# Where the survey of the weights' groups and the spread of zero points stand in the first projection of a fused attention and GPTQ block

## Chip, cores and metric

One core of a Trainium2 chip. The metric is the device time of one execution in microseconds; lower is better. Three runs of the kernel before gave 2293.84 to 2294.37 us, median 2293.89.

## Reference

One block over x of shape (2, 1024, 1024). The normalized input goes through causal attention (32 query heads and 8 key and value heads of 32) and, beside it, through a gated MLP whose weights are packed in 4 bits with scales and zero points by group. The result is x plus the product of the two.

```python
xn = _layernorm(x, axis=-1)
s = _L0_attn_ref(xn, wq, wk, wv, wo)          # q, k with rope; causal softmax; out @ wo
g = _silu(_L0_ffn_ref(xn, ...))
x = x + s * g

# in _L0_ffn_ref
w_gu = _dequant(qweight_gu, qzeros_gu, scales_gu, g_idx_gu)
gate, up = (inter[..., :INTER], inter[..., INTER:])   # inter = xn @ w_gu, INTER = 2752
h = jax.nn.silu(gate) * up
w_d = _dequant(qweight_down, qzeros_down, scales_down, g_idx_down)
# out = h @ w_d
# _dequant: W[i,j] = sc[g[i],j] * (wq[i,j] - (zq[g[i],j] + 1)), 4-bit wq and zq unpacked by shifts
```

The group index of a row is data. The kernel looks at it: if each row is in the group of its place and the scales lie in a safe range, a fast path multiplies by integers and applies ratios of scales to the sums; otherwise a general path runs.

## The kernel before

Each of the two batches goes through normalization, projection, attention and output projection; the MLP of both follows at the end. The change touches the first batch's projection.

`project` does 20 turns in that batch: four for the keys (two blocks of 512 tokens by two chunks of columns), then eight chunks of queries by two blocks. One call of `turned` makes a turn or two of them: eight fp32 products of 128x512 into a PSUM tile `ps_qk` (three buffers), on VectorE a multiplication (rot1, L388) and a shuffle (rot2, L390), on GpSimd two operations (L391, L392), on ScalarE a cast `rot_hi` (L394), on VectorE the rest `rot_lo` (L396), and on SyncE two stores. After each query chunk `xnT` is split in the same way into `x_hi` (ScalarE, L439) and `x_lo` (VectorE, L440), stored by SyncE. From the third chunk on, between the products, `head.rows()` makes the first head's scores `s` (L554, masks L548), whose maxima VectorE reads (L564); at the end of each half a transposition `m_ps` (L599) follows. At last `values(t)` makes eight value tiles `ps_v` (L407, two PSUM buffers), each copied by ScalarE into `v` (L410). Attention (`attend`) begins with products `st` (L661, L676), whose exponentials ScalarE takes (L686); the maxima of the next head come from `kst` and `qst`, loaded by SyncE (L508, L513).

At the end of each turn one step of the generator `look` is taken, behind the turn's last instructions: `next(side, None)` under `behind(turn)`. `look` has 12 steps: four of `survey` for the gate and up weights (zero points unpacked, negated and stored as two bytes in `z_gu`; scales tested; group indices tested), four for the down weights (`z_d`), one that spreads `z_gu` over the 128 rows of `zb_gu` by eight DRAM to DRAM copies, one that spreads `z_d` over `zb_d` by 21, one for `scales_turned` (scales transposed on TensorE, reciprocals and ratios on VectorE), and one for the flag that chooses the path. `unpack` reads `zb_gu` and `zb_d` from the first output projection on.

Within a stage a scheduling layer places the instructions of all engines: products of `values` are drawn forward or left at the end according to what it thinks ready. Each engine then works strictly in its order. A DMA is an instruction in the queue of the engine that issues it: the spread copies are ScalarE's, nearly everything else here is SyncE's. Tiles loaded in `look` have a buffer of their own; `psp` has one PSUM buffer for the transposed scales and the flag's sum.

Of the kernel before, what the change touches and what calls it, by code (L numbers as in the profile page):

```python
# [10 lines left out]
F32 = mybir.dt.float32  # L11
# [5 lines left out]
I32 = mybir.dt.int32  # L17
AF = mybir.ActivationFunctionType
ALU = mybir.AluOpType
AX = mybir.AxisListType  # L20
# [3 lines left out]
P = 128  # L24
# [12 lines left out]
def block_kernel(  # L37
# [18 lines left out]
    nc = tc.nc  # L56
    B, T, D = x.shape
# [7 lines left out]
    G_D = sc_d.shape[0]  # L65
# [13 lines left out]
    ones_f = const.tile([P, HD], F32, name="ones_f")  # L79
# [9 lines left out]
    flag = const.tile([1, 1], I32, name="flag")  # L89
# [19 lines left out]
    z_gu = dram.tile([G_GU, 2 * INTER, 2], U16, name="z_gu")  # L109
    z_d = dram.tile([G_D, D, 2], U16, name="z_d")  # L110
# [14 lines left out]
    def survey(pool, bad, sc, qz, gi, z_dram, col, tag):  # L125

        g, n = sc.shape
        rows = gi.shape[0]
        w = g * n // 8 // P
        words = pool.tile([P, w], U32, name=f"words_{tag}")  # L130
        nc.sync.dma_start(words, qz.rearrange("g n -> (g n)").rearrange("(p w) -> p w", p=P))
        z = pool.tile([P, w, 8], U32, name=f"z_{tag}")
        for j in range(8):
            nc.vector.tensor_scalar(z[:, :, j], words, 4 * j, 15, ALU.logical_shift_right, ALU.bitwise_and)
        yield
        zf = pool.tile([P, 8 * w], F32, name=f"zf_{tag}")
        nc.vector.tensor_scalar(zf, z.rearrange("p w j -> p (w j)"), -257.0, 15.0 * 257.0, ALU.mult, ALU.add)
        zc = pool.tile([P, 8 * w, 2], U16, name=f"zc_{tag}")
        for i in range(2):
            nc.vector.tensor_copy(zc[:, :, i], zf)  # L140
        nc.sync.dma_start(z_dram.rearrange("g n i -> (g n i)").rearrange("(p w) -> p w", p=P), zc.rearrange("p w i -> p (w i)"))
        yield

        scale = pool.tile([P, 8 * w], F32, name=f"scale_{tag}")
        nc.sync.dma_start(scale, sc.rearrange("g n -> (g n)").rearrange("(p w) -> p w", p=P))
        nc.vector.tensor_tensor(scale, scale, scale, ALU.mult)
        top = pool.tile([P, 8 * w], F32, name=f"top_{tag}")
        nc.vector.tensor_scalar(top, scale, SC_MAX * SC_MAX, None, ALU.is_le)
        nc.vector.tensor_scalar(scale, scale, SC_MIN * SC_MIN, None, ALU.is_ge)
        nc.vector.tensor_tensor(scale, scale, top, ALU.mult)  # L150
        nc.vector.tensor_scalar(scale, scale, -1.0, 1.0, ALU.mult, ALU.add)
        nc.vector.tensor_reduce(bad[:, col : col + 1], scale, AX.X, ALU.add)
        yield

        k = 64
        m = rows // k
        idx = pool.tile([k, m], I32, name=f"idx_{tag}")
        nc.sync.dma_start(idx, gi.rearrange("(p m) -> p m", p=k))
        at = pool.tile([k, m], F32, name=f"at_{tag}")
        nc.vector.tensor_copy(at, idx)  # L160
        wrap = pool.tile([k, m], F32, name=f"wrap_{tag}")
        nc.vector.tensor_scalar(wrap, at, 0.0, float(g), ALU.is_lt, ALU.mult)
        nc.vector.tensor_add(at, at, wrap)
        nc.vector.tensor_scalar(at, at, 0.0, float(g - 1), ALU.max, ALU.min)
        row = pool.tile([k, m], I32, name=f"row_{tag}")
        nc.gpsimd.iota(row, pattern=[[1, m]], base=0, channel_multiplier=m)
        nc.vector.tensor_scalar(row, row, 7, None, ALU.logical_shift_right)
        want = pool.tile([k, m], F32, name=f"want_{tag}")
        nc.vector.tensor_copy(want, row)
        nc.vector.tensor_scalar(want, want, float(g - 1), None, ALU.min)  # L170
        nc.vector.tensor_tensor(at, at, want, ALU.not_equal)
        nc.vector.tensor_reduce(bad[:k, col + 1 : col + 2], at, AX.X, ALU.add)
        yield

    def scales_turned(pool, psp):
        by_u = pool.tile([2 * G_GU, NF * P], F32, name="by_u")
        for u in range(2):
            nc.sync.dma_start(
                by_u[u * G_GU : (u + 1) * G_GU, : NF * P - P], sc_gu[:, u * INTER : u * INTER + NF * P - P]
            )  # L180
        tail = pool.tile([G_GU, P], F32, name="tail")
        for u in range(2):
            nc.sync.dma_start(
                tail[:, u * FTAIL : (u + 1) * FTAIL], sc_gu[:, (u + 1) * INTER - FTAIL : (u + 1) * INTER]
            )
        ps = psp.tile([P, NF, 2, G_GU], F32, name="ps_sc", tag="ps")
        for f in range(NF - 1):
            nc.tensor.transpose(
                ps[:, f].rearrange("p u g -> p (u g)"),
                by_u[:, f * P : (f + 1) * P],  # L190
                ident[: 2 * G_GU, : 2 * G_GU],
            )
        for u in range(2):
            nc.tensor.transpose(ps[:, NF - 1, u, :], tail, ident[:G_GU, :G_GU])
        inv = pool.tile([P, NF, 2, G_GU], F32, name="inv")
        nc.vector.reciprocal(inv, ps)
        nc.vector.tensor_tensor(r_gu, ps[:, :, :, : G_GU - 1], inv[:, :, :, 1:], ALU.mult)
        nc.vector.tensor_copy(l_gu, ps[:, :, :, G_GU - 1 :])
        by_g = pool.tile([G_D, D], F32, name="by_g")
        nc.sync.dma_start(by_g, sc_d)  # L200
        ps = psp.tile([P, NC, G_D], F32, name="ps_sd", tag="ps")
        for c in range(NC):
            nc.tensor.transpose(ps[:, c, :], by_g[:, c * P : (c + 1) * P], ident[:G_D, :G_D])
        inv = pool.tile([P, NC, G_D], F32, name="inv_d")
        nc.vector.reciprocal(inv, ps)
        nc.vector.tensor_tensor(r_d, ps[:, :, : G_D - 1], inv[:, :, 1:], ALU.mult)
        nc.vector.tensor_copy(l_d, ps[:, :, G_D - 1 :])

    def look(pool, psp):

        bad = pool.tile([P, 4], F32, name="bad")
        nc.vector.memset(bad, 0.0)
        yield from survey(pool, bad, sc_gu, qz_gu, gi_gu, z_gu, 0, "gu")
        yield from survey(pool, bad, sc_d, qz_d, gi_d, z_d, 2, "d")
        for g in range(G_GU):
            r0 = g * (P // G_GU)
            r1 = r0 + P // G_GU
            nc.scalar.dma_start(zb_gu[r0:r1], z_gu[g : g + 1].to_broadcast([r1 - r0, 2 * INTER, 2]))
        yield
        for g in range(G_D):  # L220
            r0 = g * 16
            r1 = r0 + 16 if g < G_D - 1 else RD
            nc.scalar.dma_start(zb_d[r0:r1], z_d[g : g + 1].to_broadcast([r1 - r0, D, 2]))
        yield
        scales_turned(pool, psp)
        yield
        one = pool.tile([P, 1], F32, name="one")
        nc.vector.tensor_reduce(one, bad, AX.X, ALU.add)
        ps = psp.tile([1, 1], F32, name="ps_bad", tag="ps")
        nc.tensor.matmul(ps, one, ones_f[:, :1], start=True, stop=True)  # L230
        nc.vector.tensor_scalar(flag, ps, 1.0, None, ALU.min)
        yield

    def unpack(pool, gu, down):
# [1212 lines left out]
    for b in range(B):  # L1447
# [5 lines left out]
        with tc.tile_pool(name="at_first", bufs=1, reuse_waits="tile") as fp, tc.tile_pool(  # L1453
            name="qkv_T", bufs=1, reuse_waits="tile"
# [4 lines left out]
            with tc.tile_pool(name="ps_s", bufs=1, space=PSUM, reuse_waits="tile") as ps_s:  # L1459
                head = Maxima(qs_dram[b], ks_dram[b], fp, ps_s, room)  # L1460
                if b == 0:
                    with tc.tile_pool(name="prep", bufs=1) as pool, tc.tile_pool(
                        name="prep_ps", bufs=1, space=PSUM
# [83 lines left out]
```

## Time and profile before

| what | us |
|---|---|
| median of three runs | 2293.89 |
| the profiled execution's own time | 2293.33 |
| its span in the profile | 2291.6 |
| TensorE busy | 2239.3 |
| VectorE, ScalarE, GpSimd busy | 1420.2, 1132.3, 792.4 |
| first product of the first projection starts | 26.9 |
| first product of the first attention starts | 220.4 |

A row of the timeline gives start, duration, engine, line, operation, tiles and count, and in brackets how long the engine was idle before it and what ended that. Rows marked ACTq and SPq are DMA instructions in the queues of ScalarE and SyncE; the duration of a merged row includes the waits between its instructions. An fp32 product shows as two passes in TensorE's rows. The table of stretches gives, for each engine, busy time and the number of instructions, then TensorE's granted clock (1.00 is full), the share of the DMA engines' time that is busy, and GB/s.

### The profile page before, as it was taken

Reading aid. Unit: us, or ns where it says so; the run is one execution under the profiler, and the core shown is the slowest. Engines: PE = TensorE matmul, PEld = TensorE weight load, DVE = VectorE, ACT = ScalarE, POOL = GpSimd, SP = SyncE. Lnnn points to the kernel's source line nnn. Section 1 sums busy time; section 2 is a strip of 40 time slices with the busy share of each in tenths; the row PEclk is TensorE's granted clock in tenths of the full one; section 3 lists DMA queues with packets and bytes.
Section 4 is the critical chain, followed back from the end, with each engine's and each line's share of the span. In section 5 each row is a group of like instructions: output and inputs, shape, how many; then the busy total and the mean of one; then the engine's idle time right before and its main releaser. Section 6 shows DMA issues by size and latency. Waiting matters only on the chain.

```text
span 2291.6 us, 30825 instructions
## 1 busy us (share of the span) xinstructions
PE 2239.3 (98%) x11313; PEld 1537.5 (67%) x11313; DVE 1420.2 (62%) x2268; ACT 1132.3 (49%) x1819; POOL 792.4 (35%) x569
## 2 busy tenths in 40 slices
PE   7989999999999999999999999999999999999998
PEld 4455555555874465555558888888877888888875
DVE  5544677773324736777722367667877777777775
ACT  2102544553223325445533455555887555556875
POOL 1303677774035427776741100000234100001362
PEclk9999999999999999999999999999999999999999
DMA  5727323122468971231319623231846655323475
GB/s 180 220 91 244 80 47 93 38 75 76 129 210 280 301 215 47 52 88 38 80 54 344 181 56 83 55 83 55 303 138 219 176 137 139 96 71 105 137 231 154
DMA packets 262183, 309.50 MB, mean 135 GB/s; under 512 B 19147, under 2 KB 197707, under 8 KB 261880
## 3 DMA queue, kind: packets, MB, share of 16 engines
q1 hardware_dynamic: 245172, 260.62, 38.4%
q0 software_dynamic: 10752, 38.02, 5.2%
q10 hardware_dynamic: 6100, 8.82, 1.2%
q8 instruction: 91, 1.49, 0.3%
q14 instruction: 68, 0.56, 0.1%
HBM read 214.58 MB, written 97.03 MB: 136 GB/s over the span
## 4 chain that ended last, share of the span: by engine, by line
PE 82%; issue 7%; POOL 6%; DVE 2%; ACT 2%; DMA 1%; SPq 0%; ACTq 0%; POOLq 0%; DVEq 0%
PE acc L1198 27%; PE acc L1079 12%; PE ps_wo L880 10%; PE st L661 7%; PE s L554 7%; PE o L708 5%; PE ps_qk L384 5%; PE l L726 3%; PE st L676 2%; PE ps_v L407 1%; POOL rot L391 1%; PE s L548 1%; POOL rot L392 1%; POOL p L821 1%; ACT p L686 1%
## 5 line engine op out<-in xcount | busy, mean ns | idle before, releaser
L1198 PE MATMUL acc<-x,w 128*128 128x512 f32 x2752 | 640.1, 393 | 1.2 <-ACT gate L1169 0.9
L1198 PEld LDWEIGHTS acc<-x,w 128*128 128x128 f32 x2752 | 512.3, 188 | 120.5 <-DVE h L1171 7.2
L564 DVE TENSOR_REDUCE mx<-s 128x1 f32<-128x512 f32 (+3 forms) x672 | 384.8, 608 | 190.3 <-PE s L554 91.7
L968 DVE TENSOR_SCALAR acc<-acc,r_gu 128x1024 f32<-128x1024 f32 x301 | 389.1, 1293 | 166.5 <-PE acc L1198 164.9
L686 ACT ACTIVATE p<-st 128x512 f32<-128x512 f32 (+3 forms) x768 | 314.7, 497 | 316.8 <-PE st L676 314.6
L966 ACT ACTIVATE acc<-acc,r_gu 128x1024 f32<-128x1024 f32 x301 | 327.4, 1088 | 231.5 <-PE acc L1198 226.7
L1182 POOL TENSOR_TENSOR h_lo<-h,h_hi 128x512 fp32r<-128x512 f32 x78 | 100.3, 1287 | 805.2 <-DVE h L1160 300.6
L821 POOL TENSOR_TENSOR p<-p 128x2048 f32<-128x2048 f32 (+3 forms) x122 | 360.0, 2955 | 9.0 <-PE o L708 4.6
L968 DVE TENSOR_SCALAR acc<-acc,r_d 128x512 f32<-128x512 f32 x320 | 241.7, 759 | 62.0 <-PE acc L1079 59.3
L966 ACT ACTIVATE acc<-acc,r_d 128x512 f32<-128x512 f32 x320 | 210.8, 663 | 61.8 <-PE acc L1079 55.0
L384 PE MATMUL ps_qk<-xnT,w_qk 128*128 128x512 f32 x512 | 236.0, 602 | 2.5 <-DVE rot L390 2.5
L880 PE MATMUL ps_wo<-oT,w_o 128*128 128x256 f32 x1024 | 232.1, 382 | 0.0
L1079 PE MATMUL acc<-h_lo,w 128*128 128x512 f32 (+1 forms) x576 | 228.9, 397 | 3.0 <-POOL h_lo L1182 2.6
L1079 PE MATMUL acc<-h_hi,w 128*128 128x512 f32 (+1 forms) x576 | 229.5, 398 | 0.7 <-ACT h_hi L1181 0.7
L880 PEld LDWEIGHTS ps_wo<-oT,w_o 128*128 128x128 f32 x1024 | 191.1, 190 | 40.9 <-issue 16.7
L708 PE MATMUL o<-p,v 128*32 128x512 f32 (+3 forms) x1536 | 162.9, 496 | 0.9 <-POOL p L689 0.9
L384 PEld LDWEIGHTS ps_qk<-xnT,w_qk 128*128 128x128 f32 x512 | 94.6, 192 | 99.8 <-issue 93.4
L689 POOL TENSOR_SCALAR_AFFINE_SELECT p<-p 128x512 f32<-128x512 f32 x128 | 80.5, 636 | 163.5 <-ACT p L686 123.0
L391 POOL TENSOR_TENSOR rot<-rot,cs 128x512 f32<-128x512 f32 x40 | 51.3, 1283 | 239.6 <-DVE rot L390 230.2
L554 PE MATMUL s<-kst,room 128*128 128x512 f32 (+3 forms) x384 | 130.4, 379 | 0.0
L1079 PEld LDWEIGHTS acc<-h_lo,w 128*128 128x128 f32 (+1 forms) x576 | 108.4, 188 | 31.0 <-POOL h_lo L1182 5.4
L1079 PEld LDWEIGHTS acc<-h_hi,w 128*128 128x128 f32 (+1 forms) x576 | 108.3, 188 | 30.6 <-issue 2.9
(163 smaller groups left out, 2405.7 us busy)
## 6 DMA issues: line engine op xcount, KB each, us to landing
w<-ng SPq DMA_DIRECT2D x86, 512.0 KB, 5.2
w<-nd SPq DMA_DIRECT2D x63, 512.0 KB, 4.0
ng<-nf POOLq DMA_DIRECT2D x42, 512.0 KB, 6.9
room<-qs SPq DMA_DIRECT2D x160, 128.0 KB, 4.0
x<-xs SPq DMA_DIRECT2D x32, 512.0 KB, 10.2
qst<-qs SPq DMA_DIRECT2D x96, 128.0 KB, 3.8
xt<-in_L_attn_x SPq DMA_DIRECT2D x16, 512.0 KB, 6.2
w_qk<-in_L_attn_wq SPq DMA_DIRECT2D x16, 512.0 KB, 5.0
```

Of the source, the lines that this page charges most:

```text
L384: nc.tensor.matmul(ps, w[:, s, :], xnT[:, s, tok], start=(s == 0), stop=(s == NS - 1))
L554: nc.tensor.matmul(s[:, c * w : (c + 1) * w], q[j][:, qt * P : (qt + 1) * P], k[:, k0:k1], start=n == 1, stop=c == n - 1 and (n > 1 or not ...
L564: nc.vector.tensor_reduce(mx[:, at, js[0] : js[0] + n, k0 // TB], s[:, : w * n].rearrange("p (j t) -> p j t", j=n), AX.X, ALU.max)
L661: nc.tensor.matmul(s[:, q0:], kst[g][:, kt * P : (kt + 1) * P], stack[g][j][:, qlo + q0 : qlo + TB], start=True, stop=False,)
L686: nc.scalar.activation(p[:, j, q0:], st[j][:, q0:], AF.Exp, scale=1.0 / math.sqrt(HD))
L708: nc.tensor.matmul(o[HD * j : HD * (j + 1), q0:], v[:, kt, HD * g : HD * (g + 1)], p[:, j, q0:], start=(kt == 0), stop=last,)
L821: what(*args)
L880: self.last = nc.tensor.matmul(ps[:, c * self.BLK : (c + 1) * self.BLK], self.ws[c0 + c][:, g, :], self.oT[:, g, t0 : t0 + self.BLK], star ...
L966: nc.scalar.mul(a, a, r)
L968: nc.vector.tensor_scalar(a, a, r, None, ALU.mult)
L1079: nc.tensor.matmul(acc[c], w[:k, c * P : (c + 1) * P], ht[:k, :], start=(f == 0 and t == 0), stop=(t == 1), skip_group_check=(f > 0),)
L1198: nc.tensor.matmul(a[:, n, :], w[i][:, g * P : (g + 1) * P], xs[t][:, g, n * TB : (n + 1) * TB], start=(g == 0 and t == 0), stop=(t == 1), ...
```

## The change

`look` is arranged anew, in 20 steps. First come the loads: `survey` and `scales_turned` issue their loads and yield, one after the other, in turns 1 to 3. Then the surveys' arithmetic, turns 4 to 11. Four steps are empty. `scales_turned` becomes a generator of two steps, turns 16 and 17; the flag follows at 18; the spread of `z_gu` comes at turn 19 and that of `z_d` at turn 20, the last.

```diff
@@ survey
+        k = 64
+        m = rows // k
         words = pool.tile([P, w], U32, name=f"words_{tag}")
         nc.sync.dma_start(words, qz.rearrange("g n -> (g n)").rearrange("(p w) -> p w", p=P))
+        scale = pool.tile([P, 8 * w], F32, name=f"scale_{tag}")
+        nc.sync.dma_start(scale, sc.rearrange("g n -> (g n)").rearrange("(p w) -> p w", p=P))
+        idx = pool.tile([k, m], I32, name=f"idx_{tag}")
+        nc.sync.dma_start(idx, gi.rearrange("(p m) -> p m", p=k))
+        yield
...
-        scale = pool.tile([P, 8 * w], F32, name=f"scale_{tag}")
-        nc.sync.dma_start(scale, sc.rearrange("g n -> (g n)").rearrange("(p w) -> p w", p=P))
...
-        k = 64
-        m = rows // k
-        idx = pool.tile([k, m], I32, name=f"idx_{tag}")
-        nc.sync.dma_start(idx, gi.rearrange("(p m) -> p m", p=k))
@@ scales_turned
+        by_g = pool.tile([G_D, D], F32, name="by_g")
+        nc.sync.dma_start(by_g, sc_d)
+        yield
...
-        by_g = pool.tile([G_D, D], F32, name="by_g")
-        nc.sync.dma_start(by_g, sc_d)
+        yield
@@ look
-        yield from survey(pool, bad, sc_gu, qz_gu, gi_gu, z_gu, 0, "gu")
-        yield from survey(pool, bad, sc_d, qz_d, gi_d, z_d, 2, "d")
+        parts = [
+            survey(pool, bad, sc_gu, qz_gu, gi_gu, z_gu, 0, "gu"),
+            survey(pool, bad, sc_d, qz_d, gi_d, z_d, 2, "d"),
+            scales_turned(pool, psp),
+        ]
+        for part in parts:
+            next(part)
+            yield
+        for part in parts[:2]:
+            yield from part
+
+        for _ in range(4):
+            yield
+        yield from parts[2]
+        yield
+        one = pool.tile([P, 1], F32, name="one")
+        nc.vector.tensor_reduce(one, bad, AX.X, ALU.add)
+        ps = psp.tile([1, 1], F32, name="ps_bad", tag="ps")
+        nc.tensor.matmul(ps, one, ones_f[:, :1], start=True, stop=True)
+        nc.vector.tensor_scalar(flag, ps, 1.0, None, ALU.min)
+        yield
         for g in range(G_GU):
...
             nc.scalar.dma_start(zb_gu[r0:r1], z_gu[g : g + 1].to_broadcast([r1 - r0, 2 * INTER, 2]))
         yield
         for g in range(G_D):
...
             nc.scalar.dma_start(zb_d[r0:r1], z_d[g : g + 1].to_broadcast([r1 - r0, D, 2]))
-        yield
-        scales_turned(pool, psp)
-        yield
-        one = pool.tile([P, 1], F32, name="one")
-        nc.vector.tensor_reduce(one, bad, AX.X, ALU.add)
-        ps = psp.tile([1, 1], F32, name="ps_bad", tag="ps")
-        nc.tensor.matmul(ps, one, ones_f[:, :1], start=True, stop=True)
-        nc.vector.tensor_scalar(flag, ps, 1.0, None, ALU.min)
         yield
```

## The prediction

> **What bounds the kernel now.** I read the page first (shares of busy time and the chain that ended last), then a table of stretches over the first projection, then TensorE's timeline there, then ScalarE's and SyncE's queues.
>
> From the page, engine shares and the chain:
>
> ```profile
> PE 2239.3 (98%) x11313; PEld 1537.5 (67%) x11313; DVE 1420.2 (62%) x2268; ACT 1132.3 (49%) x1819; POOL 792.4 (35%) x569
> PE 82%; issue 7%; POOL 6%; DVE 2%; ACT 2%; DMA 1%; SPq 0%; ACTq 0%; POOLq 0%; DVEq 0%
> ```
>
> TensorE is the bound: 2239.3 of 2291.6 us. A change can give only what TensorE sits idle or runs at a low clock, and costs what it adds to that. Stretches of the first projection and of the start of attention behind it (busy time by engine, then the granted clock):
>
> ```profile
> 26.00:82.00 56.00, 56.00 (x132) 25.29 (x131) 21.60 (x69) 6.56 (x12) 17.78 (x15) 0.97 0.42 130
> 82.00:151.00 69.00, 68.94 (x241) 38.46 (x240) 37.36 (x84) 2.99 (x5) 13.11 (x11) 1.00 0.47 147
> 151.00:173.00 22.00, 15.83 (x44) 8.24 (x42) 10.84 (x25) 3.95 (x8) 2.52 (x2) 0.77 0.41 135
> 173.00:220.00 47.00, 46.78 (x157) 28.58 (x156) 22.42 (x42) 10.66 (x21) 18.35 (x14) 1.00 0.69 245
> 220.00:226.00 6.00, 3.57 (x21) 2.55 (x20) 0.36 (x1) 3.72 (x6) 0.64 (x1) 1.00 1.05 238
> ```
>
> TensorE is full except at 151-173 (6.2 us idle, clock 0.77) and at 220-226 (2.4 us). Its timeline there:
>
> ```profile
> 154.12 0.38 PE L599 MATMUL m_ps<-ident_b,mt 128*128 128x128 bf16 x4 [1.39 <-DVE mt L588]
> 156.99 9.70 PE L384 MATMUL ps_qk<-xnT,w_qk 128*128 128x512 f32 x16 [2.49 <-DVE rot L390]
> 168.98 3.68 PE L407 MATMUL ps_v<-w_kv,xnT 128*128 128x256 f32 x8 [2.29 <-ACT v L410]
> 177.93 27.63 PE L384 MATMUL ps_qk<-xnT,w_qk 128*128 128x512 f32 x64
> 225.30 0.47 PE L554 MATMUL s<-kst,qst 128*128 128x128 f32 x2 [1.94 <-DMA qst<-qs]
> ```
>
> Undisturbed, 64 passes take 27.63 us, 0.432 each, so a turn's 16 take 6.9; after the gaps 16 took 9.70. The gaps' cause is on ScalarE: waits of 19.8 and 50.7 us, both on the DMA issues of the zero points' spread.
>
> ```profile
> 94.74 20.33 ACTq L218 DMA_DIRECT2D zb_gu<-z_gu  x8
> 115.17 0.62 ACT L394 CAST rot_hi<-rot 128x512 fp32r<-128x512 f32 x1 [19.82 <-DMA zb_gu<-z_gu]
> 121.37 45.07 ACTq L223 DMA_DIRECT2D zb_d<-z_d  x21
> 166.48 1.14 ACT L439 CAST x_hi<-xnT 128x512 fp32r<-128x512 f32 x2 [50.70 <-DMA zb_d<-z_d]
> ```
>
> A single issue of these rows takes 0.48 to 0.62 us; the rest of 65 us is waiting. For what, the built program says: SyncE and ScalarE share eight DMA semaphores in turn, and each DMA instruction waits until the former DMA on its semaphore has landed, whoever issued it. The queues show it:
>
> ```profile
> 133.29 0.37 SPq L350 DMA_DIRECT2D w_qk<-in_L_attn_wq  x1
> 137.98 0.47 ACTq L223 DMA_DIRECT2D zb_d<-z_d  x1
> 155.59 0.34 SPq L398 DMA_DIRECT2D qs<-rot_lo  x1
> 157.62 0.48 ACTq L223 DMA_DIRECT2D zb_d<-z_d  x1
> ```
>
> The second zb_d copy starts 4.7 us after the weight load that held its semaphore; the ninth, 2.0 us after the store of rot_lo that held its own. Landing times (last column, median us):
>
> ```profile
> room<-qs SPq DMA_DIRECT2D x160, 128.0 KB, 4.0
> qst<-qs SPq DMA_DIRECT2D x96, 128.0 KB, 3.8
> kst<-ks SPq DMA_DIRECT2D x48, 128.0 KB, 2.8
> zb_gu<-z_gu ACTq DMA_DIRECT2D x8, 344.0 KB, 6.0
> ```
>
> **The change part by part.** *Loads first.* Eleven small SyncE loads (0.3 to 0.6 us an issue, but for words_gu, which waits) are issued at turns 1 to 3. Six of them (words, scale, idx) move past each other and past stores of ks; SyncE is mostly idle until 60 us and TensorE runs without a gap to 151. The third w_qk load, issued at 22 us before, now stands behind turn 3's store (about 54 us); it is first used in turn 9, at 26.9 + 8 x 6.87 = 82 us, and lands in 5. Nothing, with 23 us of cover.
>
> *Surveys three turns later, turned scales at turns 16 and 17, flag at 18.* The same VectorE instructions in other turns; GpSimd's two iotas (0.14 us) move with them. VectorE has 5.6 us of work in a turn with rows (rotation 1.4, rot_lo 0.7, x_lo 0.7, four maxima of 0.69) against TensorE's 7.8, but the reciprocals (2.35 and 1.20) now fall among these turns, and the flag's matmul stands in TensorE's order behind a sum that is itself behind a rot_lo. Below: 0. Above: some five gaps like the 1.39 us one for m_ps, 8 us. I take 3.
>
> *The 29 zero-point copies at turns 19 and 20.* Moving them frees 151-173: 1.39 + 2.49 + 2.29 = 6.2 us idle; 9.70 - 6.9 = 2.8 of cold passes; 3.68 - 8 x 0.22 = 1.9 of cold value passes (0.22 is 7.93 us for 36 later). The 2.4 us wait for qst goes too, those loads being issued during the new stall. Gain 13.3.
>
> At their new place ScalarE's order is: rot_hi of turn 19, 8 zb_gu, rot_hi of turn 20, 21 zb_d, two x_hi, then all eight copies of v. Only two value tiles fit in PSUM, so TensorE's third value product waits for the first copy of v. Let T be the end of turn 19 on TensorE. TensorE still has turn 20 (6.9), four m_ps passes (0.4), two value tiles (16 x 0.22 = 3.5 each) and the first st products (1.28 + 0.33): it stops at T + 15.9. In the turns shown, rot_hi starts 4.2 us after its products end (shuffle, two GpSimd steps of 1.26). From there, by the semaphores that the built program names:
> - copy 1 issues at 0 and lands at 6.0; SyncE's fourth qst load waits for it, and four issues later (0.42 each) one leaves at 7.7 that lands at 11.5;
> - copy 4 waits for that, and lands at 17.5; a kst load waits for it, and the third after it leaves at 18.8 and lands at 21.6;
> - copy 7 waits for that, and lands at 27.6; a room load waits for it, and lands at 31.6;
> - the third zb_d waits for that; 19 issues of 0.62 end at 43.4. Copies 8 and 9 of zb_d wait for turn 20's stores, which are due before: turn 20's rot_hi runs at about 26.
> Two x_hi (1.1) and a copy of v (0.4) make 44.9. TensorE goes on at T + 4.2 + 44.9 = T + 49.1: **a stall of 33.2 us**. Nothing hides it: VectorE has no rows left, and the first exponentials stand behind v. Three landings of zb_gu lie on this chain; one of 4 or 8 us, as loads beside it land, makes 27 or 39.
>
> After it: 2.8 us of cold clock as after the old gap, and ScalarE's table load (1.28) and first exponentials, which before ran beside the kst products, hold TensorE about 1.3.
>
> From the first products of attention on, TensorE's instructions stand in the same order to the end, and its idle time at 226-300 is 0.85 us: no slack takes up the delay. Loads done early could win 2 us there at most.
>
> Sum: 33.2 + 2.8 + 1.3 + 3.0 - 13.3 = **+27.0 us**. On the profiled execution: span 2291.6 + 27.0 = 2318.6, plus the 1.7 outside it (2293.33 - 2291.6) is 2320.3; the median of the runs, 2293.89, is 0.6 above that execution: 2321.
>
> **Two rules of the Trainium skill against these rows.** Row: ScalarE held for 20.33 and 45.07 us by 29 copies. "DMA: Bandwidth & Descriptors", section "Issuing engines are not separate DMA queues", says that issuing from several engines saves only the sequencer's issue time, usually small. By that the copies hold ScalarE 29 x 0.62 = 18 us, with the cast, x_hi and v 20.1; the stall is 8.4 and the sum +2.2. The same page says that a semaphore wait happens on the issuing sequencer; the rows show that here, so I take the chain. Row: 16 passes at 9.70 instead of 6.9. "TensorE: Matmul & The Clock Gate", Part 1, has half rate for about 3.4 us after idling: an estimate of 1.7 us lost. The row decides, 2.8; by the rule the sum were 25.9.
>
> **The rivals.** *A: the semaphores do not bite* (SyncE's loads land sooner than zb_gu asks for theirs), and only the issues hold ScalarE for 18 us: +2.2, 2296, and -2 (2292) without the VectorE gaps and the exponentials' wait: not slower. It decides where the copies hold ScalarE less than about 20 us. For: the copies are small. Against: both holds of before. 5%. *B: the old holds come back whole*, 20.3 + 45.1 with the cast between: ScalarE frees v 1.5 us after T + 4.2 + 66.0, the stall is 55.8 and the sum +50, 2344. Against: the 45 us held two waits, for a weight buffer (121.4 to 138.0) and for a rot_lo behind late maxima (to 157.6), and neither stands there now. 8%. *C: the moved copies and the loads share the 16 DMA engines*, 0.69 busy on average before and 1.05 at 220-226; landings of 8 us make +33, 2327. This is inside my range.
>
> **How the numbers follow.** A difference below 0.2% (4.6 us) is not told from none. Stall with its chain, C included: 87%, from +15 (landings 4, no VectorE gaps, early loads help) to +38; its likeliest value is 2321. A's 5% divides into 2% within 0.2%, 3% faster. B 8%. Slower: 95%. Eight in ten: 2305 to 2336.
>
> **What would show it.** In the profile after: no gap at 151-173 and clock 1.0 there; one TensorE gap of 27 to 39 us before a ps_v of L421, ended by the copy of v on ScalarE; zb_gu's eight issues spread over about 25 us and zb_d's 21 over some 14, at about 0.62 each; qst loads of SyncE broken by waits; no qst wait at the start of attention. Wrong if ScalarE issues all 29 in under 20 us (A), if the zb_d issues again take 45 (B), if v's copies stand ahead of them, or if gaps on maxima or ps_bad exceed 8 us.

## Result and the profile after

Four runs of the changed kernel gave 2325.64 to 2328.28 us, median **2325.85**; four of the kernel before, beside them, 2294.13. The ratio is 1.0141, 95% interval 1.0126 to 1.0156: the change costs 31.7 us. The profiled execution after has a span of 2323.6 us (before: 2291.6), so the two traces differ by 32.0.

The page after, engine shares and the chain that ended last:

```profile
PE 2235.8 (96%) x11313; PEld 1536.1 (66%) x11313; DVE 1415.8 (61%) x2268; ACT 1133.1 (49%) x1819; POOL 792.5 (34%) x569
...
PE 77%; issue 7%; POOL 6%; DMA 4%; DVE 2%; ACT 2%; SPq 1%; ACTq 0%; POOLq 0%; DVEq 0%
```

TensorE has the same number of instructions and is busy 3.5 us less than before (2239.3). All of the loss is idle time, and the chain now holds 4% of DMA where it had 1%.

The stretches of the first projection and the start of attention (the engines stand in the order TensorE, its weight loads, VectorE, ScalarE, GpSimd):

```profile
26.00:82.00 56.00, 56.00 (x135) 25.65 (x135) 18.57 (x47) 6.61 (x12) 17.80 (x15) 0.99 0.46 143
82.00:151.00 69.00, 66.11 (x200) 32.88 (x198) 43.63 (x117) 9.71 (x17) 20.38 (x17) 1.00 0.54 183
151.00:173.00 22.00, 21.34 (x79) 11.15 (x78) 15.58 (x28) 2.28 (x4) 6.40 (x6) 1.00 0.25 96
173.00:220.00 47.00, 20.45 (x76) 12.24 (x74) 9.07 (x24) 2.89 (x5) 6.27 (x5) 0.77 0.83 245
220.00:260.00 40.00, 27.59 (x124) 23.46 (x125) 3.96 (x8) 8.45 (x19) 0.64 (x1) 0.80 0.18 54
```

The hole at 151-173 is filled and its clock is 1.00 instead of 0.77. In its place 173-260 has 39 us without a busy TensorE. Lines of TensorE's timeline there, and its waits in the whole projection (total, times, longest us):

```profile
175.70 0.19 PE L234 MATMUL ps_bad<-ones_f,one 128*1 128x1 f32 x2 [1.88 <-DVE one L232]
...
195.15 0.40 PE L690 MATMUL st<-mrow,ones_b 32*128 32x512 bf16 x4
230.86 23.39 PE L421 MATMUL ps_v<-w_kv,xnT 128*128 128x256 f32 x96 [35.31 <-ACT v L424]
...
256.60 0.44 PE L675 MATMUL st<-room,room 128*128 128x384 f32 x1 [1.50 <-ACT p L700]
```

```profile
PE ps_v L421 <- ACT v L424: 35.3, 1, 35.3
PE ps_bad L234 <- DVE one L232: 1.9, 1, 1.9
PE st L675 <- ACT p L700: 1.5, 1, 1.5
PE s L568 <- DVE mx L578: 1.4, 2, 0.8
PE s L568 <- DVE mrow L615: 1.3, 1, 1.3
PE m_ps L613 <- DVE mt L602: 1.1, 2, 0.8
```

One wait of 35.3 us, ended by the first copy of `v`, carries the loss. What ScalarE does meanwhile, and SyncE beside it:

```profile
184.28 26.48 ACTq L240 DMA_DIRECT2D zb_gu<-z_gu  x8
210.86 0.62 ACT L408 CAST rot_hi<-rot 128x512 fp32r<-128x512 f32 x1 [25.97 <-DMA zb_gu<-z_gu]
214.90 14.46 ACTq L245 DMA_DIRECT2D zb_d<-z_d  x21
229.40 1.14 ACT L453 CAST x_hi<-xnT 128x512 fp32r<-128x512 f32 x2 [17.92 <-DMA zb_d<-z_d]
230.44 0.64 ACT L424 COPY v<-ps_v 128x256 f32<-128x256 f32 x2
```

```profile
186.62 11.75 SPq L527 DMA_DIRECT2D qst<-qs  x16
198.41 5.57 SPq L522 DMA_DIRECT2D kst<-ks  x8
204.03 11.15 SPq L527 DMA_DIRECT2D room<-qs  x16
```

ScalarE computes next to nothing from 184.9 to 229.4. The eight copies of `zb_gu` leave one by one over 26.5 us, the 21 of `zb_d` over 14.5, and only then come `x_hi` and `v`. SyncE's 16 loads of `qst`, most of them 0.3 to 0.5 us of issue each, take 11.75. No gap before a product that reads `qst` is left at the start of attention.

What the copies wait for stands in the trace itself, which keeps for each DMA the semaphore that it waits for and signals, and the times of the signals. SyncE and ScalarE share eight semaphores, and each copy waits for the one that it will signal itself. All eight copies that were held for over 0.1 us (the last six of `zb_gu`, the first two of `zb_d`) left within 0.03 us of the landing of the SyncE load that had used their semaphore before. Six of them:

| copy | left at us | load that had its semaphore, issued at | that load landed at |
|---|---|---|---|
| third `zb_gu` | 192.35 | `qst`, 187.51 | 192.33 |
| fourth | 195.57 | `qst`, 191.77 | 195.55 |
| sixth | 203.27 | `kst`, 199.54 | 203.25 |
| seventh | 207.93 | `kst`, 203.56 | 207.91 |
| eighth | 210.29 | `room`, 207.65 | 210.26 |
| first `zb_d` | 214.90 | `room`, 210.98 | 214.87 |

So ScalarE, at its copies, keeps step with SyncE's queue of loads.

### The profile page after: what moved, and what is told of

Read it like the earlier page. It is cut to its first block, busy times and chain, and to the rows that moved or that the text cites. A ratio compares the mean times of both kernels' runs of the same rounds, so it can differ in the third digit from the quotient of the medians.

```text
span 2323.6 us, 30823 instructions
## 1 busy us (share of the span) xinstructions
PE 2235.8 (96%) x11313; PEld 1536.1 (66%) x11313; DVE 1415.8 (61%) x2268; ACT 1133.1 (49%) x1819; POOL 792.5 (34%) x569
## 4 chain that ended last, share of the span: by engine, by line
PE 77%; issue 7%; POOL 6%; DMA 4%; DVE 2%; ACT 2%; SPq 1%; ACTq 0%; POOLq 0%; DVEq 0%
PE acc L1212 27%; PE acc L1093 11%; PE st L675 7%; PE s L568 6%; PE ps_wo L894 5%; PE o L722 5%; PE ps_qk L398 5%; PE l L740 3%; PE ps_v L421 2%; PE st L690 2%; PE s L562 1%; POOL p L835 1%; POOL rot L405 1%; POOL rot L406 1%; DMA x<-xs 1%
## 5 line engine op out<-in xcount | busy, mean ns | idle before, releaser
L408 ACT CAST rot_hi<-rot 128x512 fp32r<-128x512 f32 x40 | 24.7, 618 | 247.4 <-POOL rot L406 212.0
L1093 PEld LDWEIGHTS acc<-h_hi,w 128*128 128x128 f32 (+1 forms) x576 | 108.3, 188 | 30.6 <-issue 2.9
```

Source lines behind the costliest of these rows:

```text
L1093: nc.tensor.matmul(acc[c], w[:k, c * P : (c + 1) * P], ht[:k, :], start=(f == 0 and t == 0), stop=(t == 1), skip_group_check=(f > 0),)
```

## Experiments

Three accounts were tested. H: ScalarE is held because the 29 spread copies (the expectations also call them read-backs) wait for earlier transfers, and the copies of `v` stand behind them. D: the bytes of the spread copies load the DMA engines at the wrong time. R: the rest of the change (loads, surveys, turned scales, flag at other turns) costs it. Times of one group share their runs of the kernel before: 2293.88 us in the first group (four kernels), 2294.04 in the second (four), 2294.22 in the third (two).

### 1. The same copies at the same turns, issued by GpSimd

```diff
-            nc.scalar.dma_start(zb_gu[r0:r1], ...)
+            nc.gpsimd.dma_start(zb_gu[r0:r1], ...)
...
-            nc.scalar.dma_start(zb_d[r0:r1], ...)
+            nc.gpsimd.dma_start(zb_d[r0:r1], ...)
```

> The changed kernel with the 29 spread copies issued by GpSimd at the same turns 19 and 20; nothing else differs. Theory H (ScalarE is held by the copies' waits, and the copies of v stand behind them): the 35.3 us gap before the third value tile goes, what is left of the change's gaps is 5.7 us of VectorE's and 1.5 at the first exponentials, so about 2294.1 - 13.3 + 7.2 = 2288 us (2284 to 2293). Theory D (the copies' bytes load the 16 DMA engines, and that makes the loss): same bytes at the same turns, so most of the loss stays, 2315 to 2326. Theory R (the early loads and late surveys make it): 2326.

Measured: 2289.17 us, ratio to before 0.9974 (0.9966 to 0.9982); 36.7 us less than the kernel after. The gap before `ps_v` is gone. GpSimd's queue, and the stretch in which the copies move:

```profile
184.07 4.12 POOL L240 DMA_DIRECT2D zb_gu<-z_gu  x8
...
191.30 1.51 POOL L245 DMA_DIRECT2D zb_d<-z_d  x3
194.01 0.49 POOL L245 DMA_DIRECT2D zb_d<-z_d  x1 [1.20 <-DMA zb_gu<-z_gu]
```

```profile
184.00:206.00 22.00, 22.00 (x96) 17.97 (x95) 2.04 (x4) 2.49 (x6) 16.87 (x32) 1.00 0.94 312
```

The eight copies of `zb_gu`, which took ScalarE 26.5 us to issue, take GpSimd 4.1. The DMA engines are busier than in the kernel after (0.94 of their time and 312 GB/s, against 0.83 and 234 GB/s at 184-229 there), and TensorE is full at clock 1.00 all the same. This ends D: the bytes at that place leave no gap in TensorE. Where the profile names a wait of GpSimd's among these, it is for its own copies (the `zb_d` row ended by a `zb_gu`), never for a load of SyncE's; by the trace, GpSimd's DMAs signal eight semaphores that SyncE and ScalarE do not use.

### 2. The same, issued by SyncE

```diff
-            nc.scalar.dma_start(zb_gu[r0:r1], ...)
+            nc.sync.dma_start(zb_gu[r0:r1], ...)
```

(and `zb_d` alike)

> The changed kernel with the 29 copies issued by SyncE, the queue of nearly all other DMAs. H: ScalarE is free, no gap before the values; the copies and SyncE's loads then stand in one order, so what can be late is the first qst loads of attention: 2285 to 2296 us. D: 2315 or more. R: 2326.

Measured: 2296.61 us, ratio 1.0011 (1.0003 to 1.0020), 0.6 above the range of H. SyncE's queue, and the longest of TensorE's waits:

```profile
196.81 13.75 SPq L245 DMA_DIRECT2D zb_d<-z_d  x21
...
212.62 2.64 SPq L522 DMA_DIRECT2D kst<-ks  x4
215.36 7.73 SPq L527 DMA_DIRECT2D qst<-qs  x16
```

```profile
PE s L568 <- DMA qst<-qs: 8.5, 4, 3.1
```

Nothing of `v` is late. Late is what stands behind the copies on SyncE, the loads of `qst`, and the products that read them wait 8.5 us in four pieces. The place of the loss moves with the queue that carries the copies.

### 3. The same bytes in three copies

```diff
-        for g in range(G_GU):
...
-            nc.scalar.dma_start(zb_gu[r0:r1], z_gu[g : g + 1].to_broadcast([r1 - r0, 2 * INTER, 2]))
+        nc.scalar.dma_start(
+            zb_gu.rearrange("(g r) n i -> r g (n i)", r=16),
+            z_gu.rearrange("(o g) n i -> o g (n i)", o=1).to_broadcast([16, G_GU, 4 * INTER]),
+        )
```

(and `zb_d` in two)

> The changed kernel with the same bytes spread by three copies from ScalarE in place of 29 (one for zb_gu, two for zb_d), at the same turns. By issue time alone (3 issues of about 0.6 us) ScalarE is not held and it is about 2288 us. H with the chain of shared semaphores: fewer links, but the loads that wait for the one large copy, and the zb_d copy behind them, remain; a gap of 15 us or somewhat more before the third value tile, 2303 to 2312. D: the bytes decide, 2320 to 2326.

Measured: 2314.58 us, ratio 1.0092 (1.0075 to 1.0109), 2.6 above the range of H and below that of D. ScalarE:

```profile
184.76 0.65 ACTq L237 DMA_DIRECT2D zb_gu<-z_gu  x1
191.97 0.62 ACT L409 CAST rot_hi<-rot 128x512 fp32r<-128x512 f32 x1 [6.60 <-POOL rot L407]
216.23 0.54 ACTq L242 DMA_DIRECT2D zb_d<-z_d  x1
...
219.03 1.14 ACT L454 CAST x_hi<-xnT 128x512 fp32r<-128x512 f32 x2 [26.44 <-DMA zb_d<-z_d]
```

The gap before `ps_v` is still 24.5 us. Three instructions, under 2.5 us of issue together, still hold ScalarE until 219, where 29 held it until 229: after the second `rot_hi` the first copy of `zb_d` stands from 192.6 to 216.2. So the hold is no price per issue. By the semaphores in this trace, that copy waits for a `room` load that landed at 216.21, and a `qst` load ahead of it in SyncE's queue was held for 8.3 us, until the one large transfer of `zb_gu` landed at 197.52, 12.8 us after its issue.

### 4. The kernel before with only the copies moved to turns 19 and 20

```diff
-        for g in range(G_GU):
...
-        for g in range(G_D):
...
         nc.vector.tensor_scalar(flag, ps, 1.0, None, ALU.min)
         yield
+        for _ in range(8):
+            yield
+        for g in range(G_GU):
...
+        for g in range(G_D):
...
```

> The kernel before with one part of the change alone: its spread copies moved to turns 19 and 20 (eight empty steps before them), loads, surveys, scales and flag where they were. H: the same kind of gap before the third value tile, somewhat shorter as the loads stand differently among the copies (25 to 33 us), none of the VectorE gaps beside the late scales: 2309 to 2320 us. R: no change from before, 2294. D: 2315 to 2326.

Measured: 2312.78 us, ratio 1.0082 (1.0066 to 1.0099). TensorE's waits and ScalarE:

```profile
PE ps_v L409 <- ACT v L412: 25.9, 1, 25.9
```

```profile
183.22 18.96 ACTq L228 DMA_DIRECT2D zb_gu<-z_gu  x8
202.28 0.62 ACT L396 CAST rot_hi<-rot 128x512 fp32r<-128x512 f32 x1 [18.44 <-DMA zb_gu<-z_gu]
202.30 16.55 ACTq L233 DMA_DIRECT2D zb_d<-z_d  x21
```

The move of the copies alone makes 18.9 of the 31.7 us. Most of the rest, 12.8, is a hold that is shorter here (19.0 and 16.6 instead of 26.5 and 14.5; the gap is 9.4 less): SyncE has 23 loads to issue beside the copies of `zb_gu`, where the kernel after has 41.

### 5. The kernel after with its copies past the last turn

```diff
         nc.vector.tensor_scalar(flag, ps, 1.0, None, ALU.min)
         yield
+        for _ in range(2):
+            yield
         for g in range(G_GU):
```

> The kernel after with two more empty steps ahead of the copies, so that the 29 read-backs are issued by ScalarE after the last turn, outside the block that ties them behind a turn; the order of the engines then spreads them, in groups of 2 to 6, into ScalarE's stream between the roundings, all ahead of the copies of v. H (ScalarE is held by copies that wait for earlier transfers, and the copies of v stand behind): no group is long, nothing of v comes late, the gap of 35.3 us before ps_v goes, and about 2283 to 2290 us are left, with only the short gaps of VectorE (1 to 2 us each at ps_sd and ps_bad). D (the bytes of the read-backs load the DMA engines and delay what attention needs): the bytes and the part of the kernel in which they move are unchanged, so 2315 or more. R (the moved loads, surveys and turned scales cost it): unchanged too, 2315 or more.

Measured: 2282.48 us, ratio 0.9947 (0.9933 to 0.9961): 43.4 us below the kernel after and 11.6 below the kernel before, with every other part of the change in it (0.5 below the range of H). The copies are ScalarE's as before; the scheduling layer, no longer told to keep them behind a turn, drew them forward: they stand between 71 and 187 us, not between 184 and 229. Part of ScalarE's rows:

```profile
168.44 3.20 ACTq L247 DMA_DIRECT2D zb_d<-z_d  x4
176.57 0.62 ACT L410 CAST rot_hi<-rot 128x512 fp32r<-128x512 f32 x1 [7.52 <-POOL rot L408]
176.58 0.48 ACTq L247 DMA_DIRECT2D zb_d<-z_d  x1
177.10 0.61 ACT L455 CAST x_hi<-xnT 128x512 fp32r<-128x512 f32 x1
```

Groups of one to four stand in the gaps of 6 to 11 us that ScalarE has between casts, and all are issued before the first copy of `v`. TensorE waits 1.7, 1.3, 0.8 and 0.4 us. With R unchanged in it, this ends R as the cause of the 35 us. As the bytes moved to earlier times too, it is the first experiment that ends D, not this one.

### 6. The two holds apart

```diff
-        for _ in range(4):
+        for g in range(G_GU):
+            r0 = g * (P // G_GU)
+            r1 = r0 + P // G_GU
+            nc.scalar.dma_start(zb_gu[r0:r1], ...)
+        yield
+        for _ in range(4):
             yield
```

(the copies of `zb_gu` are at turn 12, those of `zb_d` stay at turn 20, by ScalarE)

> The kernel after with the 8 read-backs of zb_gu issued ahead of the wait of four steps (turn 12), those of zb_d where they were (turn 20), both by ScalarE. H: the hold splits in two. The zb_gu hold then falls where projections are still to come and rot_hi is late by some us at most; the zb_d hold stands alone ahead of the last x_hi and the copies of v: 14 us of issue there against two free banks of ps_v (16 passes, 3.5 us each pair) leave a gap of 8 to 14 us before ps_v, so about 2296 to 2304 us. If the holds were a fixed sum wherever they stand: the gap stays near 35 us and 2325. D: the same bytes, 2315 or more. R: 2315 or more.

Measured: 2306.83 us, ratio 1.0055 (1.0040 to 1.0071), 2.8 above the range of H. The two holds on ScalarE:

```profile
120.83 7.04 ACTq L230 DMA_DIRECT2D zb_gu<-z_gu  x8
...
203.41 18.14 ACTq L245 DMA_DIRECT2D zb_d<-z_d  x21
```

```profile
PE ps_v L421 <- ACT v L424: 14.4, 1, 14.4
PE ps_sd L206 <- DVE l_gu L202: 3.4, 1, 3.4
```

At turn 12 the same eight copies hold ScalarE for 7.0 us and no product waits for it. The hold of `zb_d` alone, taken as 14 from the trace after, was 18.1, and the gap 14.4, also above H's 8 to 14; a wait of 3.4 for the reciprocals of the turned scales was not foreseen. A hold is no property of its copies: it can't be carried from one place to another.

### 7. Everything but the copies in turns 1 to 8, copies by GpSimd

```diff
-            yield
-        for part in parts[:2]:
-            yield from part
-        for _ in range(4):
-            yield
-        yield from parts[2]
+        next(gu)
+        yield
...
+        next(d)
+        next(d)
+        yield
+        next(turned)
+        yield
+        for _ in turned:
+            pass
...
-            nc.scalar.dma_start(zb_gu[r0:r1], ...)
+            nc.gpsimd.dma_start(zb_gu[r0:r1], ...)
```

> The kernel after with loads, surveys, turned scales and the flag all taken in turns 1 to 8, ahead of the work on the logits' rows, and the read-backs issued by GpSimd at turns 19 and 20. H: no hold on ScalarE, no gap before ps_v; the turned scales may wait for their loads at turn 8 (a gap of 2 to 6 us at ps_sd), and the late turns lose their gaps at ps_bad and m_ps: 2286 to 2293 us. R (the place of the loads, surveys and turned scales is what costs): packed more tightly it should cost more than the kernel after, over 2326 us. D: 2315 or more.

Measured: 2289.92 us, ratio 0.9980 (0.9973 to 0.9987). TensorE waits 2.6 us at `ps_sd`, 2.4 for `m_ps`, 1.6 at the first exponentials. Packing R into the first turns does not cost more than spreading it (2289.17 in the first experiment), as R would have had it.

### 8. The fourth experiment with GpSimd as issuer

```diff
-            nc.scalar.dma_start(zb_gu[r0:r1], ...)
+            nc.gpsimd.dma_start(zb_gu[r0:r1], ...)
```

(on top of the fourth experiment, and `zb_d` alike)

> The kernel before with only the 29 read-backs moved to turns 19 and 20, where they are issued by GpSimd; beside the run that had the same with ScalarE (2312.8 us), it differs by the issuing engine alone. H: the gap of 25.9 us before ps_v goes, and so does what the old place of the copies cost in the early turns: 2283 to 2289 us. D: the same bytes at the same time, 2312 us. That GpSimd's own additions (the rotated sum) come late behind its issues: a gap at the projections of turns 19 and 20 of up to 10 us, 2295 us.

Measured: 2286.50 us, ratio 0.9963 (0.9950 to 0.9977), 26.3 below the fourth experiment, whose kernel differs in the issuing engine alone. No rotated sum of GpSimd came late enough to show as a gap.

### 9. The copies of `v` by VectorE

```diff
-                nc.scalar.copy(v[:, t, :], ps)
+                nc.vector.tensor_copy(v[:, t, :], ps)
```

> The kernel after with the eight copies of v made by VectorE, which has little to do there; the read-backs stay with ScalarE at turns 19 and 20. H (what costs is what stands behind the read-backs on ScalarE): the gap of 35.3 us before ps_v goes, since no copy of v stands behind any more, and the next thing behind the hold comes late instead: the exponentials. TensorE runs out of projections of v at about 216 us (195.5 and 96 passes of 0.22), the hold ends at about 230.5, then come the table (1.3) and a first exponential (0.5): a gap of about 16 us before an st. Together 31.7 less 35.3 less 2.3 of cold passes, and 16 more: about +10, or 2304 us, 2299 to 2309. D (the transfers keep TensorE waiting by themselves): a gap of some 35 us stays, 2318 or more. R: 2315 or more.

Measured: 2303.34 us, ratio 1.0042 (1.0026 to 1.0057). TensorE, then ScalarE:

```profile
186.72 27.79 PE L421 MATMUL ps_v<-w_kv,xnT 128*128 128x256 f32 x128
...
233.35 0.69 PE L675 MATMUL st<-room,room 128*128 128x384 f32 x1 [16.54 <-ACT p L700]
```

```profile
183.77 27.93 ACTq L240 DMA_DIRECT2D zb_gu<-z_gu  x8
211.80 0.62 ACT L408 CAST rot_hi<-rot 128x512 fp32r<-128x512 f32 x1 [27.41 <-DMA room<-qs]
215.50 14.71 ACTq L245 DMA_DIRECT2D zb_d<-z_d  x21
230.25 1.14 ACT L453 CAST x_hi<-xnT 128x512 fp32r<-128x512 f32 x2 [17.84 <-DMA zb_d<-z_d]
```

The hold on ScalarE is as long as in the kernel after (47.6 us from the first copy to the end of `x_hi`; 46.3 there), yet the products of `v` run without a gap. The next thing behind the hold is late instead: the exponentials, 16.5 us. This is the sharpest of the runs: the 29 copies are untouched, and the loss is set by what stands behind them in ScalarE's order. The row of `rot_hi` also names the other side: its wait was ended by a `room` load, a transfer of SyncE's queue, although the cast itself reads nothing of it.

### 10. The kernel before with its copies past the last turn

```diff
-        for _ in range(8):
+        for _ in range(10):
             yield
         for g in range(G_GU):
```

(on top of the fourth experiment)

> The kernel before with the 29 read-backs put after the last turn, issued by ScalarE, so that the order of the engines spreads them in groups of 1 to 5 between its roundings; loads, surveys, turned scales and flag stay where before has them. H: no gap before ps_v, none of the gaps that the loads' late turns brought at ps_bad and ps_sd, and without the stall that the read-backs made in the early turns of the kernel before: 2280 to 2286 us, level with or 1 to 2 us below the kernel after with its read-backs spread the same way (2282.5). R (the change's new places of loads, surveys and scales are worth something by themselves): 3 us or more above that, 2285.5 or more. D: 2294 or more.

Measured: 2281.89 us, ratio 0.9947 (0.9933 to 0.9961): the fastest of all. Here the copies stand between 50 and 165 us. In the projection and at the start of attention TensorE waits 1.5, 0.7 and 0.4 us, no more:

```profile
PE m_ps L601 <- DVE mt L590: 1.5, 1, 1.5
PE s L556 <- DVE mx L566: 0.7, 2, 0.5
PE o L710 <- POOL p L691: 0.4, 1, 0.4
```

It lies 12.3 us below the kernel before and 0.6 below the fifth experiment, which has the whole rearrangement besides; the runs of the two overlap (2280.49 to 2282.75, and 2282.07 to 2283.50). The new places of loads, surveys and scales gain nothing by themselves. The pair with GpSimd as issuer says the same: the first experiment, with the rearrangement, lies 2.7 us above the eighth, without it, and their runs overlap too.

## Why the prediction was right

The likeliest case came: the stall before `ps_v`. Its terms against the trace after:

| step | predicted us | measured us |
|---|---|---|
| stall before ps_v | 33.2 | 35.3 |
| cold passes behind it | 2.8 | 2.3 (23.39 - 96 x 0.22) |
| first exponentials | 1.3 | 1.5 |
| gaps on VectorE | 3.0 | 5.7 (1.9 + 1.4 + 1.3 + 1.1) |
| old stall gone | -13.3 | -13.3 (counted in the trace before) |
| sum | +27.0 | +31.5 (span +32.0, medians +31.7) |

- *The chain of waits: right in kind, in its length partly luck.* Counted from the first copy of `zb_gu` (184.28): the fourth was to leave at 11.5 and left at 11.3; the seventh at 21.6 and left at 23.7; turn 20's `rot_hi` about 26, and it ran at 26.6; the last of `zb_d` was to be out at 43.4 and was at 45.1; the first copy of `v` was to end at 44.9 and ended at 46.5. That each held copy waits for a load of SyncE's is shown above.
- *The other half of the chain is not borne out.* Three loads of SyncE's were to wait for copies that land in 6.0 us each. Of SyncE's 40 loads from 186.6 us on, two were held by a copy, for 0.13 us together. The page's median of 6.0 us stood on one copy of the eight; by the signals of their semaphores the other seven landed in 3.2 to 4.5 us in the trace before, and all eight in 3.6 to 5.2 in the trace after. With 4 us the prediction's own sum has a stall of 27. What made up for it is a term it had too small, SyncE's own pace: the 40 loads take 28.6 us, where issues of 0.42 make 17. Their issues add up to 24.2 (eight took 0.8 to 2.1 us; why is not shown), and 2.5 went in waits for SyncE's own transfers. So two errors cancelled, and the 33.2 came closer than its working deserved. In the first experiment, without any of the 29 copies on SyncE's semaphores, the same loads take 30.6 us: the copies are not needed for that pace. A version with the semaphores dealt out differently on the same two engines was not tried.
- *The cold passes* behind the stall cost 2.3 us, between the 2.8 read from the old row and the 1.7 estimated by the clock rule that the prediction weighed.
- *The term of the sum furthest off* is the gaps on VectorE: 5.7 us, within the bounds of 0 to 8 but nearly twice the 3 taken. The largest is the one that the step named, the flag's matmul behind its sum (1.88). With GpSimd as issuer these gaps stay (1.9, 1.4, 1.3 and 1.1 us in the first experiment); with the copies drawn forward on ScalarE they shrink to 1.7, 1.3 and 0.8 (fifth). So they belong to the order of the instructions around them, not to the new turns alone.
- *The gain.* Moving only what made the old stall gives 12.3 us (tenth experiment), against 13.3 in the sum; a wait of 1.5 us for `m_ps` that the sum counted as gone is there again.
- *Loads first: nothing.* The stretch 26-82 is full. With the copies out of the way the whole rearrangement costs 0.6 us (fifth against tenth experiment) or 2.7 (first against eighth), and the runs of each pair overlap.
- *Rival A* (only issues hold) falls: ScalarE was held for 26.5 and 14.5 us, where 29 issues of 0.62 make 18. The rule weighed there (the Trainium skill, "DMA: Bandwidth & Descriptors", section "Issuing engines are not separate DMA queues") says that issuing from several engines saves only issue time. As a price for the choice of the engine that is far too low here: 29 issues make 18 us, and the choice alone was worth 36.7, by the waits in front of the copies and by what stood behind them.
- *Rival B* (20.3 and 45.1 come back whole) falls: the 45 shrank to 14.5, as its two waits were left behind, while the 20.3 grew to 26.5.
- *Rival C* (landings of 8 us) falls: the copies landed in 3.6 to 5.2 us, and the first experiment moves the same bytes beside the same loads without a gap before `ps_v`.

## What to carry to other kernels

In this kernel a DMA instruction costs the engine that issues it above all its wait, not its bytes. Before moving one, list what it waits for (the semaphore that it shares with DMAs of other queues included) and what stands behind it on that engine, to the next instruction that a critical engine reads. Here a block of 29 copies ahead of the last copies out of PSUM opened a gap of 35 us; the same copies from GpSimd, or as single issues and short groups in ScalarE's gaps, opened none before `ps_v`. The second was the faster by 4.6 us (eighth and tenth experiments) and 6.7 (first and fifth); of that, TensorE's waits in the traces account for a half to two thirds. Do not carry the length of such a hold from one place to another; it belongs to the sequence of DMAs around it. And look at what a median of landing times stands on before building a chain from it.

## What the runs showed beside this

The eight copies of `zb_gu` took 4.1 us to issue on GpSimd, and on ScalarE 7.0 (sixth experiment), 19.0 (fourth), 20.3 (kernel before), 26.5 (after) and 27.9 (ninth), at the same bytes. Fewer and larger copies did not help in proportion: with 3 instead of 29 the gap before `ps_v` went from 35.3 to 24.5 us. And with the DMA engines busy for 0.94 of the time, at 312 GB/s (first experiment), TensorE was busy for all of the 22 us at a clock of 1.00.
